# Layer one's source products by quarters, with the second norm moved from layer one to layers two and three

## The chip, the cores and the metric

One core of a Trainium2 chip runs the whole program. The metric is the device time of one execution in microseconds; the runs of a kernel on one chip lie within about 4 us of each other. In the traces, PE is TensorE (matmul), PEld its weight loads, DVE VectorE, ACT ScalarE, POOL GpSimd, SPq the queue on which SyncE issues transfers.

## The reference, cut to what matters

Sixteen graphs ("batches") of 1024 nodes and 128 features. For each: a first graph layer with a norm, then four layers on the same adjacency and a second norm.

```python
def _layer(nodes, adj, ws, bs, wd, bd, wn, bn, wu, bu):
    src_agg = einsum('bjv,bij->biv', nodes @ ws + bs, l2norm(adj, 2))
    dst_agg = einsum('bjv,bji->biv', nodes @ wd + bd, l2norm(adj, 1))
    self_rep = nodes @ wn + bn
    return tanh(concatenate([src_agg, self_rep, dst_agg], 2) @ wu + bu)

x = layernorm(x + first_gnn(x, adj))
x = layernorm(x + four_layers(x, adj))      # the "second norm"
```

## The kernel before: the parts that the change and the argument touch

Both aggregations of a layer are products of messages (128 features by 1024 nodes) with a 1024 x 1024 matrix: the column-scaled adjacency `a` for the destination part, the row-scaled transposed one `at` for the source part. Seen as 2 x 2 quarters, such a product can be made of seven quarter products and some sums and differences, in place of eight. Layers two to four do so for both parts; layer one of batches 1 to 15 did it for the destination part (`DST`) alone. TensorE works in two column halves, and one step of the loop issues one product to the upper half and one to the lower: a **pair**. Hooks are pieces of other work recorded before a given pair.

```python
# layer one; 32 pairs
upper = [
    (Z1, True, own(1, 1)), (Z0, True, own(1, 0)),
    (Z1, False, [src(1, 1, j) for j in range(2, NB)]),
    (A, True, prod("M1", DST)), (Bk, True, prod("M2", DST)), (A, True, prod("M3", DST)),
    (Z0, False, prod("Z21", DST) + [src(1, 0, j) for j in range(NB)]),
]
...  # `lower` alike
# what else is recorded in layer one of batches 1 to 15: the second norm of the batch before
w = {"ys": summed(f"y{nm}")}                      # tag "acc"
hooks = {0: begin1, 7: scale1, 12: centre1, 17: squares1, 19: rstd1,
         22: lambda: combine_1(yt), 25: end1, 28: lambda: combine(2, yt, Q)}
...
# layer two: its partial sums e12 have the tag "acc" too (a pool with one buffer)
for i in ALL:      # squares and row sums of the next adjacency: ScalarE, VectorE, GpSimd
    hooks[5 + 2 * i if i < 3 else 4 + 3 * i] = lambda i=i: sums(n, a2, st, (i,))
```

`T` and `Q` are the quarter differences of `a` and `at`, made by `combine` (VectorE, 128 x 2048 each). `begin1` transposes the second norm's input and sums it, `centre1`, `squares1` and `rstd1` are its steps with a small TensorE product before the first and the last of them, `end1` scales and stores. The next adjacency was loaded at pair 19, once the last row pieces were transposed.

## Time and profile before

| | before |
|---|---|
| time, median of 3 runs | 2503.48 us (2502.62 to 2503.82) |
| TensorE busy, span of the trace | 99% of 2500.9 us |
| one batch without a hole | 153.3 us |
| VectorE busy in layer one | 26.6 of 31.5 us |
| holes before layer three's messages | nine of fifteen batches, 5.0 us in all |

Two stages of one batch of the kernel before, layers one and two, with the busy time (and instructions) of each engine, in the order of the columns that the first line names:

```profile
core 0: us, PE busy (x) PEld busy (x) DVE busy (x) ACT busy (x) POOL busy (x), PEclk, DMA share, GB/s
...
820.00:851.50 31.50, 31.50 (x154) 12.24 (x152) 26.61 (x29) 12.66 (x25) 5.48 (x2) 1.00 0.65 115
851.50:881.00 29.50, 29.50 (x138) 11.51 (x136) 21.08 (x20) 16.55 (x29) 12.53 (x5) 1.00 0.62 120
```

TensorE fills both stages. VectorE, in layer one, has under 5 us left. Two quarter differences of `at` (2.3 us each) and the sums of the source messages (1.7 us more) would have to be added there, some 6.3 us, and the two differences that it does make there come too late: they could not simply be added.

### The profile page before, as it was taken

To read this page: it belongs to the slowest core of one execution; us is meant where nothing else is said; L and a number is where in the kernel's file an instruction comes from. 1 tells how busy PE (TensorE), PEld (TensorE's weight loads), DVE (VectorE), ACT (ScalarE), POOL (GpSimd) and SP (SyncE) were. 2 spreads that over 40 slices of the span, in tenths; PEclk is the share of its full clock that TensorE was granted. 3 is DMA by queue.
4 is the path that set the end of the run, shared out by engine and by line. 5 is a ranking of instruction groups with operands and counts; after the bars stand their busy time and mean duration, and the time that the engine had idled before them with its cause. 6 is when DMAs were issued, how large, how long until landed. Compare 5 with 4: busy or idle time off the path is not lost.

```text
span 2500.9 us, 30299 instructions
## 1 busy us (share of the span) xinstructions
PE 2482.5 (99%) x11693; PEld 1044.9 (42%) x11693; DVE 1658.2 (66%) x2030; ACT 836.3 (33%) x1554; POOL 509.4 (20%) x205
## 2 busy tenths in 40 slices
PE   8999999999999999999999999999999999999999
PEld 5443344433444344443434434334443344433444
DVE  5858566585765757667576675766758567585643
ACT  5314233142331514324143241433414333142411
POOL 4411204012130211302113030130311203112000
PEclk9999999999999999999999999999999999999999
DMA  8527154271543615436163451725417254271410
GB/s 203 106 49 145 47 101 99 57 144 35 101 103 68 128 34 111 98 74 119 43 122 79 90 102 47 136 61 102 96 50 146 52 101 100 52 144 40 93 24 9
DMA packets 361871, 219.63 MB, mean 88 GB/s; under 512 B 148928, under 2 KB 332992, under 8 KB 361728
## 3 DMA queue, kind: packets, MB, share of 16 engines
q1 hardware_dynamic: 360960, 215.35, 42.1%
q0 software_dynamic: 768, 2.36, 0.3%
q8 instruction: 92, 1.51, 0.3%
q14 instruction: 51, 0.42, 0.1%
HBM read 199.17 MB, written 18.46 MB: 87 GB/s over the span
## 4 chain that ended last, share of the span: by engine, by line
PE 85%; SPq 4%; DMA 4%; DVE 2%; ACT 2%; issue 1%; POOL 0%; POOLq 0%; ACTq 0%; DVEq 0%
PE m L695 34%; PE z L695 25%; PE pt L507 15%; PE pa L183 8%; SPq L235 3%; DMA a<-in_adj_dram 2%; PE pw L183 2%; DMA out_dram<-y 1%; DVE e L668 1%; DMA raw<-in_L_gnn_ws_dram 0%; SPq L456 0%; ACT sq L252 0%; ACT sq L249 0%; DVE cols L251 0%; DVE at L466 0%
## 5 line engine op out<-in xcount | busy, mean ns | idle before, releaser
L382 POOL TENSOR_TENSOR rs<-ve,mhalf 128x32 f32<-128x32 f32 x30 | 162.8, 5427 | 1363.9 <-DVE ve L380 1363.9
L695 PE MATMUL m<-T,S 128*64 128x512 f32 x1008 | 395.8, 593 | 0.0
L695 PE MATMUL z<-at,t 128*64 128x512 f32 x1224 | 383.7, 592 | 0.0
L695 PE MATMUL m<-a,t 128*64 128x512 f32 x1008 | 366.5, 594 | 0.0
L695 PE MATMUL m<-Q,S 128*64 128x512 f32 x768 | 339.2, 593 | 0.0
L695 PE MATMUL m<-at,t 128*64 128x512 f32 x828 | 311.0, 592 | 0.0
L510 DVE TENSOR_TENSOR t<-pt,wm 128x512 f32<-128x512 f32 x256 | 175.1, 689 | 166.4 <-PE pt L507 165.7
L256 POOL TENSOR_TENSOR acc<-acc,sq 128x1024 f32<-128x1024 f32 x90 | 220.3, 2447 | 143.3 <-ACT sq L252 139.8
L695 PE MATMUL z<-a,S 128*64 128x512 f32 x504 | 228.3, 593 | 0.0
L695 PE MATMUL z<-a,t 128*64 128x512 f32 x504 | 226.8, 592 | 0.0
L695 PE MATMUL z<-T,t 128*64 128x512 f32 x504 | 226.8, 592 | 0.0
L340 DVE TENSOR_TENSOR a<-a,cinv 128x512 f32<-128x512 f32 x250 | 156.6, 692 | 97.7 <-DMA cinv<-dr 95.2
L461 ACT ACTIVATE a<-a,rinv 128x256 f32<-128x256 f32 x480 | 198.2, 495 | 54.8 <-DMA a<-in_adj_dram 42.6
L507 PE MATMUL pt<-wm,f1T 128*128 128x256 f32 x768 | 213.7, 383 | 0.1
L183 PE MATMUL pa<-a,xn 128*64 128x512 f32 x960 | 208.6, 592 | 0.0
L695 PE MATMUL z<-at,S 128*64 128x512 f32 x444 | 202.6, 593 | 0.0
L695 PEld LDWEIGHTS m<-Q,S 128*64 128x64 f32 x768 | 104.1, 137 | 210.7 <-issue 210.1
L595 ACT COPY e<-m 64x512 f32<-64x512 f32 x63 | 36.6, 581 | 449.0 <-PE m L695 448.6
L695 PEld LDWEIGHTS m<-T,S 128*64 128x64 f32 x1008 | 117.8, 137 | 161.1 <-issue 160.5
L695 PE MATMUL z<-Q,t 128*64 128x512 f32 x384 | 172.6, 592 | 0.0
L695 PEld LDWEIGHTS z<-at,t 128*64 128x64 f32 x1224 | 120.7, 137 | 120.0 <-issue 111.5
L695 PEld LDWEIGHTS m<-a,t 128*64 128x64 f32 x1008 | 110.0, 137 | 126.4 <-issue 121.9
(197 smaller groups left out, 3762.8 us busy)
## 6 DMA issues: line engine op xcount, KB each, us to landing
a<-in_adj_dram SPq DMA_DIRECT2D x120, 512.0 KB, 12.6
a<-in_adj_dram SPq DMA_DIRECT2D x480, 128.0 KB, 4.1
wm<-wsave SPq DMA_DIRECT2D x16, 512.0 KB, 3.9
xn<-in_x_dram SPq DMA_DIRECT2D x124, 64.0 KB, 2.1
wm<-wsave SPq DMA_DIRECT2D x31, 256.0 KB, 3.5
xs<-in_x_dram SPq DMA_DIRECT2D x60, 128.0 KB, 3.6
cinv<-dr SPq DMA_DIRECT2D x30, 256.0 KB, 5.2
dinv<-dr SPq DMA_DIRECT2D x30, 256.0 KB, 5.1
```

Source lines behind the costliest of these rows:

```text
L183: nc.tensor.matmul(out[s], x[:, s], y, start=start, stop=stop)
L235: nc.sync.dma_start(ov[g, :, ks], ys[g * C:(g + 1) * C, ks])
L256: nc.gpsimd.tensor_add(acc, acc, sq)
L340: engine.tensor_mul(a[:, i, s], a[:, i, s], cinv[:, s])
L382: nc.gpsimd.tensor_tensor(rstd, ve, mhalf[:, :n], ALU.pow)
L461: nc.scalar.activation(st[:, k], st[:, k], AF.Copy, scale=rinv[:, q * QB + k:q * QB + k + 1])
L507: nc.tensor.matmul(pt[:, q], f[:, i * P:(i + 1) * P], wm[:, 1 + c], start=(k == 0), stop=(k == nch - 1))
L510: nc.vector.tensor_add(t[j][:, o:o + 2].rearrange("p k a v c -> p k (a v c)"), pt, wm[:, 0][:, None, :].to_broadcast([P, 2, 2 * P]))
L595: nc.scalar.copy(e0[high], A[high])
L668: nc.vector.tensor_add(e0[high], e0[high], e1[high])
L695: nc.tensor.matmul(o, x, y, start=start, stop=stop)
```

## The change

Its intent: save two pairs of products in every layer one by treating the source part as the destination part is treated; make room on VectorE there by moving the second norm of the batch before into layers two and three; and for that, load a third row piece earlier (into the buffers of the squares), give the norm a buffer apart from `acc`, load the next adjacency earlier and draw its squares closer together.

```diff
-        for part in (DST, SRC) if l else (DST,):
+        for part in (DST, SRC):
             nc.vector.tensor_sub(S[3][:, :, part], X[0, 0][:, :, part], X[1, 0][:, :, part])
 ...  (all message sums for both parts)
         if l == 0:
             upper = [
                 (Z1, True, own(1, 1)), (Z0, True, own(1, 0)),
-                (Z1, False, [src(1, 1, j) for j in range(2, NB)]),
-                (A, True, prod("M1", DST)), (Bk, True, prod("M2", DST)), (A, True, prod("M3", DST)),
-                (Z0, False, prod("Z21", DST) + [src(1, 0, j) for j in range(NB)]),
+                (A, True, prod("M1", DST)), (Bk, True, prod("M2", DST)), (A, False, prod("M1", SRC)),
+                (Z0, False, prod("Z21", DST)), (Bk, False, prod("M2", SRC)), (A, True, prod("M3", SRC)),
+                (Z0, False, prod("Z21", SRC)),
             ]
 ...  (`lower` alike: 30 pairs)
-            events = {10: m1_read, 14: m4_and_m2_read, 18: m3_and_second_half}
+            events = {8: m3_half, 12: m1_read, 20: m4_and_m2_read, 24: last_reads}
 ...  (layer one, batches 1 to 15)
-            hooks = {0: begin1, 7: scale1, 12: centre1, 17: squares1, 19: rstd1,
-                     22: lambda: combine_1(yt), 25: end1, 28: lambda: combine(2, yt, Q)}
+            hooks = {0: rows3, 3: lambda: combine(4, y, T), 5: next_rows, 7: lambda: combine(2, yt, Q),
+                     9: lambda: combine(3, yt, Q), 11: lambda: combine(4, yt, Q)}
 ...  (layer two)
+            w = {"ys": summed(f"y{nm}", "xa")}
+            sums_of_next = dict(zip((1, 2, 4, 6, 12, 15, 18, 20), map(sums_of, ALL))) if nxt else {}
+            hooks = {0: begin1, 11: centre1, 14: squares1, 17: rstd1, **sums_of_next}
 ...  (layer three: end1, with its stores, at pair 4)
 ...  (layer four: row piece 1 loaded at pair 10 into two "sq" tiles, scaled at pair 27)
 ...  (the two buffers of tag "xT" become one "xa" and one "xb")
```

More of the change, by code (lines that the diff above doesn't have):

```diff
@@ L342, in to_features @@
     def to_features(xs, name):
-        dst = two.tile([P, N], F32, tag="xT", name=f"{name}T")
+        dst = one.tile([P, N], F32, tag="xa", name=f"{name}T")
         nc.vector.transpose(dst, xs.rearrange("p k f -> p (k f)"))
@@ L416, in norm_write_act, with summed @@
         nc.scalar.activation(dst, pn, AF.Identity, bias=shift[:, q:q + 1], scale=rstd[:, q:q + 1])
-    def summed(name):
-        return one.tile([P, K, C], F32, tag="acc", name=name)
+    def summed(name, tag):
+        return one.tile([P, K, C], F32, tag=tag, name=name)
     def x1_features(b, ys, h, dst):
@@ L453, in load_rows @@
         v = adj[b, q * QB * C:(q + 1) * QB * C].rearrange("(k r) (h g j) -> h g r k j", r=C, h=NH, g=G)
-        for g in range(G):
-            for h in range(NH):
-                queue.dma_start(st[g * C:(g + 1) * C, :, h * P:(h + 1) * P], v[h, g])
+        n = QB // len(st)
+        for i, piece in enumerate(st):
+            for g in range(G):
+                for h in range(NH):
+                    queue.dma_start(piece[g * C:(g + 1) * C, :, h * P:(h + 1) * P], v[h, g, :, i * n:(i + 1) * n])
         return st
     def scale_rows(st, q, rinv):
+        n = QB // len(st)
         for k in range(QB):
-            nc.scalar.activation(st[:, k], st[:, k], AF.Copy, scale=rinv[:, q * QB + k:q * QB + k + 1])
+            row = st[k // n][:, k % n]
+            nc.scalar.activation(row, row, AF.Copy, scale=rinv[:, q * QB + k:q * QB + k + 1])
     def transpose_rows(st, q, at):
         h, o = divmod(q * QB * C, HW)
+        n = QB // len(st)
         for j in range(0, NB, NJ):
-            nc.vector.transpose(
-                at[h][:, j:j + NJ, o:o + QB * C].rearrange("p j (k c) -> p j k c", c=C),
-                st.rearrange("p k (j c) -> p j k c", c=C)[:, j:j + NJ])
+            for i, piece in enumerate(st):
+                c = slice(o + i * n * C, o + (i + 1) * n * C)
+                nc.vector.transpose(
+                    at[h][:, j:j + NJ, c].rearrange("p j (k c) -> p j k c", c=C),
+                    piece.rearrange("p k (j c) -> p j k c", c=C)[:, j:j + NJ])
     def transposed(b, h):
@@ L515, in messages @@
             return t
-        s = slice(1 if l == 0 else 0, 2)
         S = {i: one.tile([P, NJ, 2, V], F32, tag=f"S{i}", name=f"S{i}_{l + 1}_{b}") for i in (2, 3, 4)}
@@ L521, in messages @@
         S[1] = X[1, 0]
-        if l == 0:
-            nc.vector.tensor_sub(S[2][:, 0:2, 0], X[0, 0][:, 0:2, 0], X[1, 0][:, 0:2, 0])
-        for part in (DST, SRC) if l else (DST,):
+        for part in (DST, SRC):
             nc.vector.tensor_sub(S[3][:, :, part], X[0, 0][:, :, part], X[1, 0][:, :, part])
-        nc.vector.tensor_add(S[1][:, :, s], X[1, 0][:, :, s], X[1, 1][:, :, s])
-        nc.vector.tensor_sub(S[2][:, :, s], S[1][:, :, s], X[0, 0][:, :, s])
-        nc.vector.tensor_sub(S[4][:, :, s], X[0, 1][:, :, s], S[2][:, :, s])
+        nc.vector.tensor_add(S[1], X[1, 0], X[1, 1])
+        nc.vector.tensor_sub(S[2], S[1], X[0, 0])
+        nc.vector.tensor_sub(S[4], X[0, 1], S[2])
         return X, S
@@ L572, in aggregate @@
         Ck = product(f"m4_{l}_{b}")
-        Dk = product(f"m3_{l}_{b}") if l else None
+        Dk = product(f"m3_{l}_{b}")
         A, Bk = (product(f"m{i}_{l}_{b}") for i in (1, 2))
@@ L580, in own @@
             return [(w[:, c, v * V:(v + 1) * V], blocks(f[:, half(h)])) for f, c in feats]
-        def src(v, h, j):
-            return (X[v, j // NJ][:, j % NJ, SRC], at[h][:, j])
         def prod(name, part):
@@ L613, in second_half, with m3_half, m2_and_half_of_m3, last_reads @@
             squash(l, 1, e1, fT)
+        def m3_half():
+            nc.scalar.copy(e1[high], Dk[low])
+        def m2_and_half_of_m3():
+            m2_read()
+            nc.vector.tensor_add(e0[high], e0[high], e1[high])
+        def last_reads():
+            m3_read()
+            second_half()
         if l == 0:
@@ L624, in aggregate @@
                 (Z1, True, own(0, 1)), (Z0, True, own(0, 0)),
-                (Z1, False, [(S[2][:, j, SRC], at[1][:, j]) for j in range(2)] + [src(0, 1, j) for j in range(2, NB)]),
-                (Ck, True, prod("M4", DST) + [src(1, 1, j) for j in range(2)]),
-                (Z1, False, prod("Z12", DST)),
-                (Z0, False, prod("Z11", DST) + [src(0, 0, j) for j in range(NB)]),
+                (Dk, True, prod("M3", DST)), (Ck, True, prod("M4", DST)), (Z1, False, prod("Z12", DST)),
+                (Z0, False, prod("Z11", DST)), (Ck, False, prod("M4", SRC)), (Z1, False, prod("Z12", SRC)),
+                (Z0, False, prod("Z11", SRC)),
             ]
@@ L631, in m4_and_m2_read @@
                 m4_read()
-                m2_read()
-            def m3_and_second_half():
-                m3_read()
-                second_half()
-            events = {10: m1_read, 14: m4_and_m2_read, 18: m3_and_second_half}
-        else:
-            def m3_half():
-                nc.scalar.copy(e1[high], Dk[low])
+                m2_and_half_of_m3()
+            events = {8: m3_half, 12: m1_read, 20: m4_and_m2_read, 24: last_reads}
+        else:
             first_of_lower = [(Ck, True, prod("M4", DST) + prod("M4", SRC)), (Dk, True, prod("M3", DST))]
@@ L664, in first_reads @@
                 reads_of_lower[0]()
-            def m2_and_half_of_m3():
-                m2_read()
-                nc.vector.tensor_add(e0[high], e0[high], e1[high])
-            def last_reads():
-                m3_read()
-                second_half()
             events = {8: first_reads, 12: reads_of_lower[1], 16: m2_and_half_of_m3, 20: last_reads}
@@ L723, in adj_resnorm_kernel @@
     a = apool.tile([P, NB, N], F32, tag="a", name="a0")
-    w0n = two.tile([P, 2 * P], F32, tag="xT", name="w0n")
+    w0n = one.tile([P, 2 * P], F32, tag="xb", name="w0n")
     av = [adj[0, half(h)].rearrange("(g k c) i -> g c k i", g=G, c=C) for h in range(NH)]
@@ L756, in adj_resnorm_kernel @@
         if q is not None:
-            rows[q] = load_rows(0, q, places[q])
+            rows[q] = load_rows(0, q, [places[q]])
     for q in (0, 1):
-        rows[q] = load_rows(0, q, places[q])
+        rows[q] = load_rows(0, q, [places[q]])
     nc.vector.memset(mhalf, -0.5)
@@ L768, in adj_resnorm_kernel @@
     nc.gpsimd.memset(inv[:, 3 * NB:], 0.0)
-    xT = two.tile([P, N], F32, tag="xT", name="x0_T")
+    xT = one.tile([P, N], F32, tag="xa", name="x0_T")
     def to_xT(h):
@@ L821, in adj_resnorm_kernel @@
     x1n = two.tile([P, NB, D], F32, tag="sq", name="x1n0")
-    x1T = two.tile([P, N], F32, tag="xT", name="x1_0_T")
+    x1T = one.tile([P, N], F32, tag="xb", name="x1_0_T")
     dinv = one.tile([P, N], F32, tag="acc", name="dinv0")
@@ L984, in adj_resnorm_kernel, with rows3, next_rows, sums_of @@
         else:
-            nm = f"1_{b - 1}"
             t = messages(b, 0, feats, wm)
             wm = message_weights(b, 1)
-            w = {"ys": summed(f"y{nm}")}
+            w = {}
             Q = combined(b, "Q")
+            def rows3():
+                for q in (1, 0):
+                    transpose_rows(rows[q], q, at)
+            def next_rows(w=w):
+                combine_1(yt)
+                if nxt:
+                    w["a"] = load(n)
+            hooks = {0: rows3, 3: lambda: combine(4, y, T), 5: next_rows, 7: lambda: combine(2, yt, Q),
+                     9: lambda: combine(3, yt, Q), 11: lambda: combine(4, yt, Q)}
+            aggregate(b, 0, feats, t, a, at, T, Q, f1, "row", hooks)
+            a2, xs2 = w.get("a"), None
+        feats = [(f1, 0)]
+        f23 = feature(b, "f23T")
+        t = messages(b, 1, feats, wm)
+        wm = message_weights(b, 2)
+        def sums_of(i):
+            return lambda: sums(n, a2, st, (i,))
+        hooks = {}
+        if b == 0:
+            def quarters2():
+                for i in (2, 3, 4):
+                    combine(i, yt, Q)
+            hooks = {0: quarters2, 12: lambda: combine(4, y, T)}
+            hooks |= {5 + 2 * i if i < 3 else 4 + 3 * i: sums_of(i) for i in ALL}
+        else:
+            nm = f"1_{b - 1}"
+            w = {"ys": summed(f"y{nm}", "xa")}
+            sums_of_next = dict(zip((1, 2, 4, 6, 12, 15, 18, 20), map(sums_of, ALL))) if nxt else {}
             def begin1(w=w, nm=nm):
-                transpose_rows(rows[0], 0, at)
                 norm_spread(w["ys"], f4, KS)
                 w["s"] = norm_sum(w["ys"], KS, nm, back)
-            def scale1():
-                scale_rows(rows[1], 1, rinv)
             def centre1(w=w, nm=nm):
-                combine(4, y, T)
                 w["sq"] = norm_centre(w["ys"], w["s"], KS, nm)
+                if nxt:
+                    w["xs"] = load_spread(n)
             def squares1(w=w, nm=nm):
@@ L1007, in rstd1, with end1 @@
                 w["r"] = norm_rstd(w["v"], KS, nm)
-                transpose_rows(rows[1], 1, at)
-                if nxt:
-                    w["a"] = load(n)
-                    w["xs"] = load_spread(n)
-            def end1(w=w):
+            hooks = {0: begin1, 11: centre1, 14: squares1, 17: rstd1, **sums_of_next}
+        aggregate(b, 1, feats, t, a, at, T, Q, f23, "acc", hooks)
+        second_norm = w if b else None
+        if b:
+            xs2 = w.get("xs")
+        feats = [(f1, 1), (f23, 0)]
+        w = {}
+        def end1(w=second_norm):
+            if b:
                 norm_end(w["ys"], w["r"], KS)
                 store(b - 1, w["ys"], KS)
-            hooks = {0: begin1, 7: scale1, 12: centre1, 17: squares1, 19: rstd1,
-                     22: lambda: combine_1(yt), 25: end1, 28: lambda: combine(2, yt, Q)}
-            aggregate(b, 0, feats, t, a, at, T, Q, f1, "row", hooks)
-            a2, xs2 = w.get("a"), w.get("xs")
-        feats = [(f1, 0)]
-        f23 = feature(b, "f23T")
-        t = messages(b, 1, feats, wm)
-        wm = message_weights(b, 2)
-        def quarters2(b=b):
-            for i in ((2, 3, 4) if b == 0 else (3, 4)):
-                combine(i, yt, Q)
-        hooks = {0: quarters2}
-        if nxt:
-            for i in ALL:
-                hooks[5 + 2 * i if i < 3 else 4 + 3 * i] = lambda i=i: sums(n, a2, st, (i,))
-        if b == 0:
-            hooks[12] = lambda: combine(4, y, T)
-        aggregate(b, 1, feats, t, a, at, T, Q, f23, "acc", hooks)
-        feats = [(f1, 1), (f23, 0)]
-        w = {}
         def inverses3():
             inverses(n, st)
+            end1()
         def start3(w=w):
@@ L1065, in scale @@
             scale_columns(a2, w["cinv"], range(i, i + NJ), half(h))
-        hooks, between = {}, {}
+        hooks, between = {4: end1}, {}
         if nxt:
@@ L1092, in add0 @@
             def add0(w=w):
-                w["ys"] = summed(f"y0_{n}")
+                w["ys"] = summed(f"y0_{n}", "acc")
                 for h in range(NH):
@@ L1117, in rows0 @@
                 for i, q in enumerate((2, 3)):
-                    rows[q] = load_rows(n, q, place(i))
+                    rows[q] = load_rows(n, q, [place(i)])
+                rows[1] = load_rows(n, 1, [two.tile([P, QB // 2, NH * P], F32, tag="sq", name=f"rows1_{n}_{i}")
+                                           for i in range(2)])
             def end0(w=w):
                 norm_end(w["ys"], w["r"], KS)
-                w["x1"] = two.tile([P, N], F32, tag="xT", name=f"x1_{n}_T")
+                w["x1"] = one.tile([P, N], F32, tag="xb", name=f"x1_{n}_T")
                 for h in range(NH):
@@ L1137, in rows1 @@
                 w["back"] = take_back(b, kept)
-                rows[0] = load_rows(n, 0, place(0))
+                rows[0] = load_rows(n, 0, [place(0)])
             def rows2():
                 transpose_rows(rows[3], 3, at2)
-                rows[1] = load_rows(n, 1, place(1))
+                scale_rows(rows[1], 1, rinv)
             between = {0: add0, 1: spread0, 2: sum0, 3: centre0}
```

## The prediction

> **What bounds the kernel now.** I read the page first (busy shares, then the chain of the end), then the order in time of each engine through one of the sixteen batches (780 to 933 us), then the waits, then one batch that is longer than its neighbours. The page:
>
> ```profile
> PE 2482.5 (99%) x11693; PEld 1044.9 (42%) x11693; DVE 1658.2 (66%) x2030; ACT 836.3 (33%) x1554; POOL 509.4 (20%) x205
> ...
> PE   8999999999999999999999999999999999999999
> ...
> PE 85%; SPq 4%; DMA 4%; DVE 2%; ACT 2%; issue 1%; POOL 0%; POOLq 0%; ACTq 0%; DVEq 0%
> ```
>
> TensorE is busy over 90% of every slice after the first, and the chain is TensorE's own instructions; clock granted 0.999. So time = matmul work + the few gaps. What one unit of the work costs is in the order in time of TensorE, at the end of a layer one, where the two column halves of the array run as a pair:
>
> ```profile
> 823.68 1.94 PE L695 MATMUL z<-x_T,wown 128*64 128x512 f32 x8
> ...
> 844.14 0.59 PE L695 MATMUL z<-T,t 128*64 128x512 f32 x1
> 844.14 0.59 PE L695 MATMUL z<-a,t 128*64 128x512 f32 x1
> 844.57 7.04 PE L695 MATMUL z<-at,t 128*64 128x512 f32 x32
> 851.53 3.72 PE L507 MATMUL pt<-wm,f1T 128*128 128x256 f32 x16
> ```
>
> A program matmul leaves two records, so a pair (upper and lower half) is four: 32 records in 851.53 - 0.10 - 844.57 = 6.86 us, 0.857 us a pair. The 32 pairs of layer one and two small norm products fill 823.68 to 851.43 without a hole. The only holes that recur are at the start of layer three's messages, in ten of the fifteen batches; this is one:
>
> ```profile
> 726.92 0.70 PE L507 MATMUL pt<-wm,f1T 128*128 128x256 f32 x2
> 728.22 0.70 PE L507 MATMUL pt<-wm,f23T 128*128 128x256 f32 x2 [0.59 <-ACT f23T L708]
> ```
>
> Comparing the spacing there with the normal 0.43 us, they cost 0.19 to 1.07 us each, 5.0 us in all (batches last 153.3 us where it is missing, up to 154.4 where it is largest). ScalarE's order in time in that batch, and its waits over the run, show where it starts:
>
> ```profile
> 715.51 0.58 ACT L641 COPY e<-m 64x512 f32<-64x512 f32 x1 [2.71 <-DMA out_dram<-y]
> ...
> ACT e L641 <- DMA out_dram<-y: 25.5, 13, 2.9
> ```
>
> The output of the second norm leaves from the buffer that layer two's partial sums need; its four stores sit behind the 4 MB load of the next adjacency (the four issues spanned 18.38 us in that batch). ScalarE waits, its squares and copies slip, and the tanh that feeds layer three is late.
>
> [...] the trace has 0.857/4 = 214 ns, so every record removed from a full TensorE is worth that. [...] the trace has 2.28 to 2.29 us for the quarter differences. [...] at 861.07 a 2.28 us difference took 4.45 us while GpSimd's accumulation ran 860.61 to 863.38. [...] here the stores' 128-byte packets flow only from 863 us on, when the load's packets end.
>
> **The change part by part.** (a) TensorE. Before, layer one does the destination part by seven quarter products and the source part plainly: 2 own + 6 + 4 + 4 + 4 + 4 + 8 = 32 pairs. After, both parts by seven: 2 + 7 x 4 = 30. Two pairs x 0.857 = 1.71 us a batch; batch 0 has its own plain layer, so 15 x 1.71 = **25.7 us** less. All else on TensorE is the same; the four norm products move one layer on.
>
> (b) VectorE in layer one, in the clock of the batch shown (own products start 823.69, pair i starts at 823.74 + 0.856 i). The source sums grow from 1.9 to the 3.58 us that layer two shows between its last message add and the next work: done 827.37. Then in order: four 128x512 transposes (0.64 each, from the two that took 1.31) 829.9; two 128x1024 (2.29) 832.2; T4 834.4; the in-place difference 836.6; Q2 (dependent, 2.4) 839.1; Q3 841.5; Q4 843.7. TensorE asks for the transposed half at pair 10 (832.3, by its first transposes, done 831.1), T4 at 14 (835.7), Q2 at 18 (839.14), Q3 at 22 (842.6), Q4 at 26 (846.0). All fit; Q2 has no margin, so 0 to 0.3 us a batch. The second norm's 7.3 us of VectorE work (six operations of 1.2) has left this layer to make the room.
>
> (c) End of layer one. The last reads move from 12 pairs before the end to 4 (3.4 us). The chain there (add, add, add, tanh) took 2.96 us in layer two of this batch (878.35 to 881.31), plus 0.27 to see the product. Margin 0.2 us: 0 to 0.2 us a batch.
>
> (d) Layer two. The load of the next adjacency is issued when the last row pieces are transposed, at 832 and not 843, so it has landed when ScalarE gets free at 853.1; before, the squares began at 855.92 on the data. The first two rows take 4.55 us, GpSimd's first accumulation starts at about 858.2 and shuts out the last message sum until 860.5. The norm's transpose, residual add and reduction (1.15 + 1.25 + 1.25) end at 865.0; TensorE meets its small product before pair 11, at 864.65. So some 0.4 us of new gap in the fourteen batches with a next one: about 5 us. In return the stores no longer stand before layer two's buffer, ScalarE does not wait, the last chain starts about 877.6 and not 878.35, and the **5.0 us** of holes before layer three go.
>
> (e) Layer three. The stores (4,096 packets, 4.4 us in the trace) now go ahead of the small transfer that brings the column factors: about 2 us later. From there VectorE's scaling, the degree factors and the second aggregate product of the next batch follow; its last user on TensorE has 1.7 us after a VectorE wait of 1.3, so 2.9 us of room. Nothing on the path.
>
> Sum: 2503.5 - 25.7 - 5.0 + about 5 (d) + about 1.5 (b, c) = **2479 us**, 1% faster.
>
> **The rivals.** 1. VectorE becomes the bound of layer one: its work there is back to back from 824 to 844, and if each operation were 0.1 us slower than I took it, Q2 would be 1 us late. For: no margin at Q2. Against: the durations are constant in the trace (2,278 to 2,293 ns) and GpSimd, which could hold it up, has no work there any more. It would make 2503.5 - 25.7 + 15 = 2490 us or so.
> 2. Crowding in layer two: squares closer together plus the norm, with GpSimd's 2.3 us accumulations against VectorE's two-input operations. For: the 4.45 us case. Against: the two buffers of squares leave GpSimd idle between its first and second accumulation, where the residual add fits. If each batch lost 1 to 1.5 us, 2490 to 2495 us.
> 3. The stores ahead of the column factors cost more than their 2.9 us of room (small packets, waits for the norm's end). [...] Against: the queue is empty then. Each further microsecond is 15 us in all: 2490 us.
> 4. None of the new gaps appears, and all holes go: 2503.5 - 30.7 = 2473 us, the floor; nothing takes more matmuls away.
>
> **Range and chances.** The matmul saving is certain; what swings is 15 times a few tenths. From the floor less 1 to a full microsecond lost a batch: 2471 to 2489. Faster by over 2% needs 2453, 20 us under the floor: 0.01. Slower by over 2% would need 5 us of new gap in every batch: 0.01. Within 2%: 0.98.
>
> **What would show it.** TensorE's page line with 11,573 records (120 fewer) and a busy time lower by 25 us; layer one in some 25.7 us from own products to the next messages; gaps if any at pair 18 of layer one (waiting for Q) and before the small product at pair 11 of layer two (waiting for the reduction). The wait of ScalarE on the output stores gone, and the hole before layer three with it. A gap at the second aggregate product of the next batch, or a longer VectorE wait for the column factors than 6.3 us plus 2, would prove rival 3. The prediction is wrong if the batches differ from 151.6 us by more than 0.7.

## More of the kernel before

The batches' lengths are read from the chain of work in order of time, from one start of the first aggregate product to the next:

```profile
454.79 13.73 PE pa L183 x64
...
608.65 13.73 PE pa L183 x64
...
762.81 13.73 PE pa L183 x64
...
916.11 13.73 PE pa L183 x64
```

153.86, 154.16 and 153.30 us: the first two of these batches have a hole, the third has none.

## The result, and the profile after

| | before | after |
|---|---|---|
| time, median (range), same chip | 2503.05 us (2501.46 to 2503.82), 4 runs | 2473.60 us (2471.72 to 2473.83), 4 runs |
| ratio | | 0.9883 (95%: 0.9868 to 0.9898) |

A ratio here is the mean time of one kernel's fast runs over that of the other's of the same rounds, so it is not quite the ratio of the medians. The change is 1.2% faster: inside the predicted range, within the 2% that the prediction gave 0.98 to, and 5.4 us faster than its centre of 2479.

The page of the kernel after, its first line of busy times and its chain:

```profile
PE 2457.1 (99%) x11573; PEld 1037.2 (42%) x11573; DVE 1689.8 (68%) x2075; ACT 843.1 (34%) x1569; POOL 524.8 (21%) x205
...
PE 97%; DMA 1%; SPq 1%; DVE 0%; ACT 0%; issue 0%; POOLq 0%; DVEq 0%
```

There are 120 fewer TensorE records, as worked out, and the chain that ends last is TensorE to 97%, where it was 85%: the detours over the stores and ScalarE are gone. The same four starts of the first aggregate product, in the kernel after:

```profile
451.44 13.73 PE pa L183 x64
...
603.12 13.73 PE pa L183 x64
...
754.79 13.73 PE pa L183 x64
...
906.47 13.73 PE pa L183 x64
```

Every batch takes 151.67 to 151.69 us: the holes before layer three are gone. That accounts for the 28.9 us between the two traced spans (2500.9 and 2472.0). From the first of these starts to the fifteenth it is 2151.2 us before and 2123.5 after, 27.7 less: fourteen times 1.62 (153.30 - 151.68: the 1.71 of two pairs, less a new gap of some 0.1 that the last experiment removes) is 22.7, and the holes were 5.0. The stretch behind the fifteenth start, with the last batch's layer one in it, is 1.7 shorter; the start of the program took 0.5 longer. Layers one and two of one batch, columns as above:

```profile
963.60:993.20 29.60, 29.60 (x138) 11.50 (x136) 25.72 (x27) 10.60 (x22) 0.00 (x0) 1.00 0.66 133
993.20:1023.10 29.90, 29.90 (x146) 11.65 (x144) 24.24 (x25) 20.10 (x34) 18.61 (x7) 1.00 0.29 56
```

Layer one is 1.9 us shorter and VectorE is nearly as busy in it as before, 25.7 us, now of 29.6; layer two has taken most of the norm, and its stretch, 0.4 us longer, holds eight more TensorE records (the norm's two small products). Layer one on VectorE, from the last transposes to the quarter differences, and TensorE's first product with Q2:

```profile
973.44 2.33 DVE L473 STREAM_TRANSPOSE at<-a 128x1024 f32<-128x1024 f32 x2
975.69 2.24 DVE L500 TENSOR_TENSOR T<-a,T 128x2048 f32<-128x2048 f32 x1
977.86 2.28 DVE L492 TENSOR_TENSOR at<-at,at 128x2048 f32<-128x2048 f32 x1
980.17 2.29 DVE L496 TENSOR_TENSOR Q<-at 128x2048 f32<-128x2048 f32 x1
...
982.84 0.59 PE L692 MATMUL m<-Q,S 128*64 128x512 f32 x1
```

Q2's instruction ends at 980.17 + 2.29 = 982.46 and the product that needs it starts at 982.84, on its beat of 0.43 us after the one before: the chain fits with 0.38 us to spare, less the time of a signal (0.06 us: the weight load of that product starts at 982.52). And layer two, where the prediction expected a new gap: VectorE's last two message sums and the norm's last step before its small product, GpSimd's first accumulation, and the small product itself.

```profile
999.25 0.69 DVE L531 TENSOR_TENSOR S<-t 128x512 f32<-128x512 f32 x1
999.98 2.73 DVE L532 TENSOR_TENSOR S<-t,S 128x512 f32<-128x512 f32 x1
...
1005.16 1.22 DVE L356 TENSOR_REDUCE s<-y 128x32 f32<-128x1024 f32 x1
...
999.38 2.77 POOL L254 TENSOR_TENSOR acc<-sq,sq 128x1024 f32<-128x1024 f32 x1 [53.03 <-ACT sq L252]
...
1006.43 0.31 PE L183 MATMUL pm<-s,fold 128*64 128x32 f32 x4
```

The long last sum is there, as predicted: 0.69 us where GpSimd is idle (at 1033.65), it takes 2.73 here, from 999.98 to 1002.71, and GpSimd's addition, which had started 0.60 us before it, ends at 1002.15. GpSimd's own 2.77 (the later additions take some 2.4) begin, it seems, with a wait for the VectorE sum before, which ends at 999.94. But the reduction ends at 1005.16 + 1.22 = 1006.38, and the small product starts at 1006.43. That is 9.54 us after the layer's own products start, where it is 9.49 in the last batch, in which GpSimd has nothing to add: the small product is 0.05 us late, and not the 0.4 predicted.

In layer three, where the stores now stand ahead of the column factors, VectorE waits for these factors less than before, not more (kernel before, then after):

```profile
DVE a L340 <- DMA cinv<-dr: 95.2, 15, 7.5
...
DVE a L340 <- DMA cinv<-dr: 73.0, 15, 5.9
```

The factors land 24.4 us after the start of layer three's messages, 24.9 before the change (medians of fifteen batches).

### The profile page after: what moved, and what is told of

Its sections match the earlier page's. It is cut to its first block, busy times and chain, and to the rows that moved or that the text cites.

```text
span 2472.0 us, 30281 instructions
## 1 busy us (share of the span) xinstructions
PE 2457.1 (99%) x11573; PEld 1037.2 (42%) x11573; DVE 1689.8 (68%) x2075; ACT 843.1 (34%) x1569; POOL 524.8 (21%) x205
## 4 chain that ended last, share of the span: by engine, by line
PE 97%; DMA 1%; SPq 1%; DVE 0%; ACT 0%; issue 0%; POOLq 0%; DVEq 0%
PE m L692 44%; PE z L692 26%; PE pt L514 16%; PE pa L183 8%; PE pw L183 2%; DMA raw<-in_L_gnn_ws_dram 1%; SPq L458 0%; PE z L562 0%; PE pm L183 0%; DMA a<-in_adj_dram 0%; PE d L562 0%; DMA raw<-in_L_gnn_bs_dram 0%; DMA rows<-in_adj_dram 0%; DMA raw<-in_L_gnn_wn_dram 0%; SPq L131 0%
## 5 line engine op out<-in xcount | busy, mean ns | idle before, releaser
L692 PE MATMUL m<-Q,S 128*64 128x512 f32 x1008 | 446.4, 593 | 0.0
L692 PE MATMUL m<-at,t 128*64 128x512 f32 x1008 | 393.5, 593 | 0.0
L692 PE MATMUL m<-a,t 128*64 128x512 f32 x1008 | 390.6, 593 | 0.0
L692 PEld LDWEIGHTS m<-Q,S 128*64 128x64 f32 x1008 | 135.7, 137 | 270.8 <-issue 260.9
L692 PE MATMUL z<-at,S 128*64 128x512 f32 x504 | 230.1, 594 | 0.0
L692 PE MATMUL z<-at,t 128*64 128x512 f32 x504 | 226.6, 592 | 0.0
L692 PE MATMUL z<-Q,t 128*64 128x512 f32 x504 | 226.6, 592 | 0.0
L254 POOL TENSOR_TENSOR acc<-sq,sq 128x1024 f32<-128x1024 f32 x15 | 41.6, 2770 | 761.7 <-ACT sq L252 761.7
L692 PEld LDWEIGHTS m<-at,t 128*64 128x64 f32 x1008 | 120.2, 137 | 143.9 <-issue 143.9
L692 PEld LDWEIGHTS m<-a,t 128*64 128x64 f32 x1008 | 119.0, 137 | 126.1 <-issue 117.3
```

The source lines that it names most:

```text
L254: nc.gpsimd.tensor_add(acc, state["sq"], sq)
L692: nc.tensor.matmul(o, x, y, start=start, stop=stop)
```

## The experiments

Times of one call are beside runs of the kernel before on the same chip (medians 2500.5, 2501.3 and 2502.6 us in the three calls).

### Two pairs put back

```diff
-                (Z0, False, prod("Z21", SRC)),
+                (Z0, False, prod("Z21", SRC) + prod("Z21", SRC)[:2]),
 ...
-                (Z0, False, prod("Z11", SRC)),
+                (Z0, False, prod("Z11", SRC) + prod("Z11", SRC)[:2]),
```

Its output is wrong, which doesn't matter for the time.

> The changed kernel with two pairs of products put back at the end of every layer one (the result is wrong on purpose), nothing else altered. Theory (the saving is TensorE work alone, two pairs of 0.857 us in fifteen batches): 2473.6 + 25.7 = 2499.3 us, within 1.5; TensorE again 11,693 records. Rival (part of the gain comes from the order of the products or from the new places of VectorE's work, which the longer layer would keep): clearly under 2497.

Measured: 2497.67 us (12 runs, 2497.14 to 2499.91), against 2500.49 for the kernel before, ratio 0.9991 (0.9983 to 1.0000). In the order of time, three starts of the first aggregate product:

```profile
452.97 13.73 PE pa L183 x64
606.37 13.73 PE pa L183 x64
759.76 13.73 PE pa L183 x64
```

153.39 us a batch against 151.68: 1.71 for two pairs, fifteen times 25.7. The saving is TensorE work and nothing else; the rest of the change, without it, is worth the holes: 2.8 us on this chip. The time is 1.6 us under the 2499.3 that the theory gave, just outside its 1.5, and not under the rival's 2497. As 2499.3 started from the first chip's time, the batches are the better evidence.

### The kernel before, with another buffer for the second norm

```diff
-        dst = two.tile([P, N], F32, tag="xT", name=f"{name}T")
+        dst = one.tile([P, N], F32, tag="xa", name=f"{name}T")
 ...  (the other users of "xT": "xa" or "xb", as in the kernel after)
-            w = {"ys": summed(f"y{nm}")}
+            w = {"ys": summed(f"y{nm}", "xa")}
```

> The kernel before with one thing altered: the second norm works in the buffer that the changed kernel gives it, so that its output stores no longer stand before layer two's partial sums; products, order, places of norm and squares as before. Theory (the holes before layer three come from ScalarE's wait for these stores): that wait is gone, the ten holes of 0.2 to 1.07 us are gone, 2503.1 - 5.0 = 2498 us, within 1.5. Rival (the holes come from the squares and GpSimd's accumulations crowding VectorE late in layer two): they stay, 2502 to 2504.

Measured: 2498.25 us (13 runs) against 2500.49, ratio 0.9990 (0.9982 to 0.9998). In its trace seven of the nine holes are gone and two of 0.37 and 0.38 us remain (the prediction and the expectation count ten; the tenth, of 0.02 us, is none); the batches sum to 2147.0 us where the kernel before had 2151.2. ScalarE's waits at the copy that had waited for the stores, and, in one of the two batches that still have a hole, the stores on the queue and the start of the squares:

```profile
ACT e L641 <- PE m L695: 16.5, 16, 1.0
...
386.90 17.87 SPq L235 DMA_DIRECT2D out_dram<-y  x4
...
395.15 1.06 ACT L249 ACTIVATE sq<-a 128x1024 f32<-128x1024 f32 x1 [3.77 <-DMA a<-in_adj_dram]
```

The stores are as slow as ever, but nobody waits for them. What is left of the holes starts from a load of the next adjacency that arrives late (3.77 us of waiting here, 2.67 in the next batch, which has no hole; 3.52 in the other batch with a hole, and at most 3.11 in those without).

The trace of the kernel before shows the same two causes apart. Its longest waits of the copy for the stores are 2.04, 2.15, 2.23, 2.41, 2.55, 2.71 and 2.93 us, and the holes of these seven batches are 0.18, 0.30, 0.36, 0.55, 0.69, 0.86 and 1.07: each is the wait less some 1.86 us, and no batch with a shorter wait has a hole from it. The two other holes, 0.60 and 0.36, stand in the two batches in which the squares waited longest for the load (4.26 and 3.54 us) and the copy hardly for the stores (0.27 and 0.03): the same two batches that keep a hole here. So the wait for the stores caused seven holes and the late load two; the change removes both causes, as it also issues that load 11 us earlier. The load was not moved by itself in any run. On this chip the gain in time was 2.2 us and not 5.0, so that the time met the expected 2498 partly by luck. The kernel before took 2500.5 us on this chip against 2503.05 on the first, so it probably had smaller holes here, but no trace of it on this chip was taken.

### The squares at their old places

```diff
-            sums_of_next = dict(zip((1, 2, 4, 6, 12, 15, 18, 20), map(sums_of, ALL))) if nxt else {}
+            sums_of_next = dict(zip((5, 7, 9, 13, 16, 19, 22, 25), map(sums_of, ALL))) if nxt else {}
```

> The changed kernel with the next adjacency's squares at the places in layer two that they had before (pairs 5, 7, 9, 13, 16, 19, 22, 25 and not 1, 2, 4, 6, 12, 15, 18, 20). Theory (their distance is worth nothing: GpSimd's last two accumulations wait for the norm's power in both): the 0.06 us before the norm's first small product goes as GpSimd starts later, 2472 to 2474.5 us. Rival (closer together is what keeps the last accumulation in time for layer three): the column sums come late, gaps of 1 us or more at the small product early in layer three, 2488 or more.

Measured: 2474.59 us (4 runs, 2474.11 to 2475.74), ratio 0.9898 (0.9882 to 0.9913). The time is 0.1 us above what the theory allowed, and its reason failed. GpSimd did not start later (2.49 us after the own products in both kernels): a hook's pair number sets only the order of recording, and ScalarE, with nothing else to do, takes the first squares as soon as the tanh is done, in both kernels (in the kernel after the tanh runs from 994.08 to 994.80 and the first square starts at 994.71). So the small product stayed late. What changed is at the other end, in VectorE's waits:

```profile
DVE acct L265 <- POOL acc L256: 26.7, 15, 1.9
```

The column sums wait some 1.8 us a batch for GpSimd's last accumulation (28.0 us in all in the kernel before; the kernel after has no such line among its 50 longest waits). The column factors land 25.8 us after the start of layer three's messages (median) and not 24.4, and three batches, in which the second aggregate product of the next batch waits for them, are 0.3, 0.6 and 1.0 us longer. So the rival had the delay right (the column sums do come late) and its size and place wrong. Drawing the squares together buys about 1.4 us of room on that chain; its worth in time is 2 us or so, by the traced batches (2125.4 against 2123.5 us).

### The second norm back in layer one

```diff
-            hooks = {0: rows3, 3: lambda: combine(4, y, T), 5: next_rows, 7: lambda: combine(2, yt, Q),
-                     9: lambda: combine(3, yt, Q), 11: lambda: combine(4, yt, Q)}
+            hooks = {0: begin1, 3: lambda: combine(4, y, T), 5: next_rows, 7: lambda: combine(2, yt, Q),
+                     9: lambda: combine(3, yt, Q), 11: lambda: combine(4, yt, Q),
+                     12: centre1, 17: squares1, 19: rstd1, 25: end1}      # begin1: rows3, then the norm's start
 ...  (layers two and three: the norm's hooks taken out)
```

> The changed kernel with the second norm back in layer one, at the places it had in the kernel before (begun after the transposes, then pairs 12, 17, 19 and 25). Theory (layer one's VectorE chain from the message sums to the quarter differences has next to no room): 3.65 us more ahead of T4 make TensorE wait 2 us for T4, 1 us more for Q2, and some 7 us at the norm's second small product, whose reduction now stands behind all differences: 10 us or more a batch, 2600 us or more. Rival (the norm moved only to free the buffer, and VectorE is off the path in layer one): within 5 us of 2474.

Measured: 2656.01 us, one run; batches of 163.8 us, 12.1 more than the kernel after. TensorE in one layer one, then VectorE's norm behind the differences:

```profile
228.12 0.64 PE L692 MATMUL m<-Q,S 128*64 128x512 f32 x1 [0.88 <-DVE Q L496]
...
236.19 0.43 PE L183 MATMUL pv<-v,fold 128*64 128x32 f32 x4 [6.98 <-DVE v L372]
236.42 1.09 PE L692 MATMUL m<-Q,S 128*64 128x512 f32 x1
...
237.31 1.06 PE L692 MATMUL m<-Q,S 128*64 128x512 f32 x1
...
239.02 0.60 PE L692 MATMUL m<-Q,S 128*64 128x512 f32 x1
```

```profile
230.31 2.28 DVE L500 TENSOR_TENSOR Q<-at,Q 128x2048 f32<-128x2048 f32 x1
232.51 1.22 DVE L363 SCALAR_TENSOR_TENSOR y<-pm,y 128x1024 f32<-128x1024 f32 x1
234.91 1.22 DVE L372 TENSOR_REDUCE v<-sq 128x32 f32<-128x1024 f32 x1 [1.18 <-ACT sq L366]
```

Measured against the normal spacing the gaps are 1.8 us before the norm's first small product, which waits for its reduction, and 0.3 before T4's products behind it (2 expected, all for T4), 1.0 before Q2's (1 expected) and 7.3 at the second small product (7 expected). Behind the last one, after 6.98 us of idling, the products run at half pace, 0.85 to 0.89 us apart and not 0.43, for three steps, which costs 1.3 us more; full pace is back 2.6 us later (236.42 to 239.02). Behind the shorter waits of this layer, 1.60 and 0.88 us, the next step took 0.46 and 0.48 us. Where between these waits and 6.98 us the half pace sets in was not shown. So the move of the norm is what makes the products of (a) possible. VectorE's 25.7 us in the new layer one and the norm's 7.3 would be 33.0, more than the 29.6 that TensorE needs there, in whatever order. With these places for the norm, layer one loses seven times what its two pairs save.

### The kernel after once more, and two doses on VectorE

The doses put one more subtraction into the chain, with a result that is overwritten later:

```diff
             def next_rows(w=w):
+                nc.vector.tensor_sub(Q[3][:, 0], T[2][:, 0], y[0, 0][:, 0])     # 0.7: 128x512
+                nc.vector.tensor_sub(Q[3], T[2], y[0, 0])                       # or 2.3: 128x2048
                 combine_1(yt)
```

> The changed kernel once more, on the chip of these runs, so that the others have it beside them. The gaps of its trace should repeat: batches of 151.7 us, the holes before layer three gone, nothing at the second aggregate product. Both theories: 1.0 to 1.2% under the kernel before.

Measured: 2473.75 us (4 runs), ratio 0.9886 (0.9871 to 0.9901); batches of 151.66 to 151.69 us. The same as on the first chip.

> The changed kernel with one more 128x512 subtraction on VectorE in every layer one, after T4 and before the quarter differences (its result is overwritten). In the trace of the changed kernel Q2's instruction ends at 982.46 and TensorE's first product with it starts on its beat at 982.84, so the room is 0.38 us less a signal of about 0.05. Theory: 0.6 to 0.7 us more makes TensorE wait 0.3 to 0.4 us there in fifteen batches, 5 to 6 us more than the changed kernel. Rival (more room than the trace shows, as TensorE takes weights ahead or as later pairs make up for it): no change.

Measured: 2477.55 us (4 runs, 2476.46 to 2478.68), 3.8 more than the kernel after beside it (5 to 6 expected); batches of 152.01 us, 0.33 more, which is 5.0 us in fifteen.

> The same with a whole 128x2048 subtraction of 2.2 us at that place. Theory: 2.2 - 0.3 = 1.9 us of gap in fifteen batches before the products with Q2, 29 us more than the changed kernel, the saving gone. Rival: the slack of VectorE in this layer takes up part of it, under 20 us more.

Measured: 2502.07 us, one run, 28.3 more; batches of 153.61 us, 1.93 more. Q2 and the product that waits for it in this kernel:

```profile
223.37 2.29 DVE L496 TENSOR_TENSOR Q<-at 128x2048 f32<-128x2048 f32 x1
...
225.72 0.64 PE L692 MATMUL m<-Q,S 128*64 128x512 f32 x1 [1.71 <-DVE Q L496]
```

225.72 is 0.06 us after Q2's end at 225.66: that is the signal. Of 0.6 us (the small dose takes 0.60 from its start to the next instruction's) 0.33 came through, of 2.2 us 1.93: the room is 0.27 us in both, and everything beyond it is paid by TensorE in full. The expectation's rival named weights taken ahead: in the kernel after the load of Q2's product does start 0.32 us before its record (982.52 and 982.84), but it gave no more room. Rival 1 of the prediction is thus real, but stays 0.3 us away.

### The stores issued twice

```diff
                 norm_end(w["ys"], w["r"], KS)
                 store(b - 1, w["ys"], KS)
+                store(b - 1, w["ys"], KS)
```

> The changed kernel with the four output stores of the second norm issued twice in layer three (same data to the same place). Theory (the stores stand ahead of the column factors in the queue, 4.4 us of packets each time, and there are 1.6 us before TensorE, 1.4 before VectorE): the factors come 4.4 us later, the second aggregate product of the next batch waits 1 to 1.5 us in fourteen batches, 14 to 21 us more than the changed kernel. Rival (small transfers pass the stores, or the chain has more room): less than 3 us more.

Measured: 2484.78 us (4 runs, 2483.72 to 2486.45), 11.0 more than the kernel after beside it. A batch, TensorE at the second aggregate product of the next one:

```profile
465.49 1.08 PE L183 MATMUL pw<-agT,w0T 128*64 128x512 f32 x4 [0.98 <-DVE agT L433]
```

The mechanism is right and the place is right; the size was over-estimated. The column factors land 28.1 us after the start of layer three's messages (median) where the kernel after has 24.4, so the second set of stores delayed them by 3.6 us and not 4.4, and the batches are 0.8 us longer on average (152.50), with 0 to 2.3 in single ones. The batches also show the deadline itself. VectorE's first scaling of the next batch's aggregate (`agT`) costs nothing when it starts 47.55 us after layer three's messages; at 47.91 the batch is 0.34 longer and at 49.85 it is 2.27 longer, and the others, those with the squares at their old places too, lie on the same line: what exceeds 47.57 us is paid in full. In the kernel after that scaling starts at 44.9 (median; 46.3 in its worst batch), so its room is 2.7 us, and 1.3 at worst.

### The first small product one pair later

```diff
-            hooks = {0: begin1, 11: centre1, 14: squares1, 17: rstd1, **sums_of_next}
+            hooks = {0: begin1, 14: squares1, 17: rstd1, **sums_of_next}
+            ...   hooks[12]: centre1, then the sums that were at 12
```

> The changed kernel with the norm's first small product in layer two one pair later (pair 12 and not 11). Its sums are ready at 9.49 us after the layer's own products start and pair 11 comes at 9.46, so that TensorE loses 0.06 us in most batches; at pair 12 there is 0.8 us of room. Theory: that gap goes, batches of 151.6 us (151.68 in the changed kernel), 1 us less in all, too little for the times to show; no new gap, as the second small product at pair 17 had about 1 us of room. Rival: the later centring makes the second small product late, a gap of 0.1 us or more there.

Measured: 2471.76 us (4 runs, 2470.93 to 2472.36) against 2502.59, ratio 0.9876 (0.9860 to 0.9893); all fourteen batches take 151.58 to 151.59 us. The gap is gone and no other has come: 0.10 us a batch, 1.4 in all. This is the fastest version; that it beats the kernel after is shown by the batches of the traces, not by the times, whose intervals overlap.

## Why the prediction was right, and by how much it missed

Direction, mechanism and class were right; the centre was 5.4 us too slow (2479 predicted, 2473.6 measured), and the step that failed is the new gaps in the sum: about 5 us in (d), which measured 1.4, and 1.5 in (b) and (c), which measured nothing.

- **(a) TensorE, -25.7.** Right: two pairs put back cost 1.71 us a batch, and the trace has 120 records fewer. The division by four is not the pace of a record, though: on the whole array too a 128 x 512 record starts 0.43 us after the one before (32 of them in 13.90 us in batch 0), and a pair has its four records in 0.857 us because the two halves run side by side, their records starting 0.00 to 0.01 us apart. So 214 ns is a share and no pace; the sum needs the 0.857 us alone, which the run with two pairs more bears out.
- **(b) VectorE in layer one, 0 to 0.3 a batch.** The chain came out within 0.3 us of the ledger, and on the good side: Q2 was predicted 0.0 us ahead of its deadline and was 0.3 ahead. The gap is zero. The doses show that the room is 0.27 us, so a range from 0 was fair and a centre above it was not.
- **(c) The end of layer one, 0 to 0.2.** The tanh ends at 992.87 us (992.15 + 0.72) and the next messages begin at 993.24: no gap.
- **(d) Layer two, about +5.** This is the term that was mis-sized. GpSimd's first addition did hold up the last message sum (2.73 us, not 0.69), but the small product came 0.05 us late and not 0.4, and the whole loss was 0.1 us a batch. The ledger put the end of the reduction 9.81 us behind the start of the layer's own products (855.19 in the batch that it used); the trace has 1006.38 - 996.89 = 9.49. It placed GpSimd's start at 3.0 us (its own terms, 853.1 + 4.55, give 2.5, and the trace has 2.49), but GpSimd took 2.77 us and not 2.3, it seems with a wait for the sum before, so that it ended at 5.26, nearly the 5.31 forecast. The error is in what follows: from there the ledger leaves 0.85 us until the norm's transpose can begin (865.0 - 3.65 - 860.5), and the trace has 0.48 (1002.15 to 1002.63; GpSimd's ends are rough), as the next VectorE instruction, which does not read the last sum, starts 0.08 us before that sum's end at 1002.71. The norm's three steps took 3.75 us and not 3.65. With the deadline at 9.46, 0.3 us too much in all became 5 us of prediction. The other half of (d), the holes of 5.0 us, was right: they are all gone. The stores were the cause of seven of the nine; behind the two others stands the late load, a second cause that the prediction had not told apart.
- **(e) Layer three, nothing on the path.** Right that nothing is on the path, but partly by luck: the column factors were to come 2 us later, and they land 24.4 us after the start of layer three's messages where the kernel before has 24.9 (medians). The stores do delay them: the transfer ahead of them takes 2.0 us from issue to landing, and not 1.4. But that transfer is issued 1.3 us earlier, as the column sums no longer wait 1.9 us a batch for GpSimd's last accumulation (0.9 us of the gain is lost to a GpSimd power that takes 3.8 us and not 2.9); this gain is not in the prediction. So the room did not shrink from 2.9 to 0.9: it is 2.7 us.
- **Rivals.** 1 and 3 were shown to be real limits with 0.3 and 2.7 us of room (1.3 in the worst batch). 2 (crowding in layer two) showed its first sign, 0.1 us a batch. 4, the floor of 2473, is nearly what happened.

## What to carry to other kernels

When one engine is busy to 99%, a change is worth the work that it takes off that engine plus the holes that it closes (22.7 and 5.0 us here, of 27.7 over fourteen batches), and its risk is counted in the room that each chain has at its deadline; read that room from the trace to a tenth of a microsecond, and measure it with a dose of known size. A ledger of deadlines should step by the time from one start to the next, not by durations: some 0.4 us too much at one step made a forecast of 5 us of gaps where the runs have 1.4. A buffer that is shared with slow stores can hold up an engine that has nothing to do with them (ScalarE here, by up to 2.9 us); giving it another name closed seven of nine holes without moving any work.

## What else the traces show

- GpSimd's additions held up a VectorE instruction with two SBUF inputs (a 0.69 us sum took 2.73), but a GpSimd power did not. In the kernel before, a power of 5.43 us (5.42 at 797.22, where VectorE ran nothing beside it) went on while two VectorE instructions with two SBUF inputs, started 3.8 and 4.4 us into it, took their normal 0.69 and 2.28 us:

```profile
840.74 5.43 POOL L382 TENSOR_TENSOR rs<-ve,mhalf 128x32 f32<-128x32 f32 x1 [38.09 <-DVE ve L380]
...
844.56 0.69 DVE L612 TENSOR_TENSOR e<-e 128x512 f32<-128x512 f32 x1
845.17 2.28 DVE L485 TENSOR_TENSOR at<-at,at 128x2048 f32<-128x2048 f32 x1
```

- In the kernel before, the GpSimd powers took 5.4 us for 128 x 32 values and 2.9 for 128 x 16; the latter became 3.8 in the kernel after, where it met a VectorE scaling of 1.22 us with two SBUF inputs.
- An fp32 product leaves two records in these traces (two pairs, four products, in fifteen batches made 120), 0.43 us apart for 512 columns, on the whole array as on a half, so that one pair of 128 x 64 by 512 products, side by side, took 0.857 us.
